# Border between two stages: last core stores from ScalarE's queue, layer 0's gate two turns behind the transposes of x, square roots one turn later

## The chip, the cores and the metric

The kernel runs on one core of a Trainium2 chip. The time is the device time of an execution in microseconds. A core has a matrix engine (TensorE, PE in the profile), a vector engine (VectorE, DVE), an activation engine (ScalarE, ACT), a general engine (GpSimd, POOL) and a queue engine that only issues transfers (SyncE, SP). Each of them takes its own instructions in the order in which the program lists them, and they wait for one another through semaphores. TensorE writes to PSUM[...]; the other data lie in SBUF, and the large arrays in the memory outside.

## The reference

The input x is an array of 384 x 384 positions with 128 channels. Two layers follow each other.

```python
# layer 0
z = layernorm(x)
left  = (z @ Wl + bl) * sigmoid(z @ Wlg + blg)
right = (z @ Wr + br) * sigmoid(z @ Wrg + brg)
core  = einsum('bikh,bjkh->bijh', left, right)
x1 = x + sigmoid(x @ Wg + bg) * (layernorm(core) @ Wout + bout)
# layer 1
left = x1 @ W_left + b_left + x1 @ W_eq + b_eq
out  = left * sum_j(x1 @ W_right + b_right) * sigmoid(x1 @ W_gate + b_gate)
y = layernorm(out @ W_out + b_out + x1)
```

All data are 32-bit floats. The gate `sigmoid(x @ Wg + bg)` of layer 0 needs nothing but x.

## The kernel before

The work is done in three stages, and the order of every engine's instructions is the order of the program (every instruction goes through `seq`, which keeps it).

Stage 1 normalizes x, multiplies it by the four weights of layer 0 (L249), applies the gates (L251, L253) and writes left and right, channel by channel, to `lr_d`. The last two of its result tiles are kept in SBUF (`kept`).

Stage 2 runs over the 128 channels h. `load_h` (L86, L87) brings the channel's left and right from `lr_d`, two channels ahead; `fill` (L316) copies the kept part on GpSimd. Nine pairs of matmuls (L325) make the 384 x 384 core of the channel in PSUM, in one of two buffers of three banks. ScalarE copies it to `ct` (L331) and squares it into `sq` (L333); VectorE adds both to the running sums `csum` and `csq` (L334, L335). Last, SyncE stores `ct` to `core_d` (L337). `ct` has three buffers.

Stage 3 runs over turns t, and each turn works on several rows at once, each at another step. `row(d)` is the row d turns behind. The steps of a row i that matter here are

- turn i: TensorE transposes the row of x (three transposes into `pxt`, L418) and ScalarE copies them to `xT` (L420);
- turn i + 1: TensorE multiplies `xT` by `wg0` into `pg` (L410) and ScalarE makes the gate `gT` (L412);
- turn i + 16: GpSimd multiplies the row's core by the reciprocal deviation into `cs` (L426);
- turn i + 18: TensorE multiplies `cs` by the output weights into `pr` (L453), and VectorE applies the gate and adds x (L454, L456).

The later steps (L469 to L507, up to turn i + 26) are layer 1. Within a turn the gate of the row before stands ahead of the transposes of the row itself. `pg`, `pxt`, `pq`, `pr`, `pg2` and `pl` take turns in four PSUM banks (`bank`). `gT` and `xT` have 20 buffers each. For the first 16 turns TensorE has nothing to do but gates and transposes.

Rows of x come four at a time (`load_x`, L365, four buffers): four loads are issued before turn 0, and one more at each fourth turn. Before turn 5, `rstd` is listed: VectorE makes the variances from `csum` and `csq` (L387 to L389), ScalarE takes their square roots (L390), VectorE makes the reciprocals (L393 to L396), and GpSimd's queue stores them to `rstd_d` (L397). Right behind it come the first two loads of core rows (`load_core`: L370 for `core_d`, L372 for `rstd_d`), both on SyncE. ScalarE's square root and its sigmoid need different function tables, so a table is loaded on either side of the roots.

Of the kernel before, what the change touches and what calls it, by code (L numbers as in the profile page):

```python
# [14 lines left out]
P = 128  # L15
# [4 lines left out]
def triangle_then_gated_row_kernel(ctx: ExitStack, tc: tile.TileContext, a: dict, out: bass.AP):  # L20
# [9 lines left out]
    nc = tc.nc  # L30
# [3 lines left out]
    H = a["L0_conv_Wl"].shape[1]  # L34
# [12 lines left out]
    core_d = dpool.tile([N, H, N], F32, name="core_d")  # L47
    rstd_d = dpool.tile([N, N], F32, name="rstd_d")

    def seq(ins):  # L50

        return tc.keep_in_program_order(ins)
# [21 lines left out]
    with ExitStack() as ctx2:  # L74
# [4 lines left out]
        def load_h(h):  # L79

            if h < H:
                t = inp.tile([P, NB, N, 2], F32, tag="lrh", name="lrh")
                src = lr_d[h].rearrange("(b p) i s -> p b (i s)", p=P)
                i1 = 2 * G * (NG - KEEP)
                dst = t.rearrange("p b i s -> p b (i s)")
                seq(nc.sync.dma_start(out=dst[:, :NB - 1], in_=src[:, :NB - 1]))  # L86
                seq(nc.sync.dma_start(out=dst[:, NB - 1, :i1], in_=src[:, NB - 1, :i1]))  # L87
                loaded2[h] = t
# [215 lines left out]
        with tc.tile_pool(name="p2out", bufs=3, side="right", reuse_waits="tile") as op, \  # L304
             tc.tile_pool(name="p2sq", bufs=2, side="right", reuse_waits="tile") as qp, \
             tc.tile_pool(name="p2ps", bufs=2, space=PSUM, reuse_waits="tile") as ps:
            csum = spool.tile([P, NB, N], F32, name="csum")
            csq = spool.tile([P, NB, N], F32, name="csq")
            seq(nc.vector.memset(csum, 0.0))
            seq(nc.vector.memset(csq, 0.0))  # L310

            def fill(h):

                if h < H:
                    for (kb, ig), lrt in kept.items():
                        seq(nc.gpsimd.tensor_copy(loaded2[h][:, kb, ig * G:(ig + 1) * G, :], lrt[:, h]))  # L316

            fill(0)
            for h in range(H):
                fill(h + 1)  # L320
                t = loaded2.pop(h)
                pc = ps.tile([P, NB, 512], F32, tag="pc", name="pc")
                for kb in range(NB):
                    for ib in range(NB):
                        seq(nc.tensor.matmul(  # L325
                            pc[:, ib, :N], lhsT=t[:, kb, ib * P:(ib + 1) * P, 0], rhs=t[:, kb, :, 1],
                            start=(kb == 0), stop=(kb == NB - 1),
                        ))

                ct = op.tile([P, NB, N], F32, tag="ct", name="ct")  # L330
                seq(nc.scalar.copy(ct, pc[:, :, :N]))  # L331
                sq = qp.tile([P, NB, N], F32, tag="sq", name="sq")
                seq(nc.scalar.activation(sq, ct, AF.Square))  # L333
                seq(nc.vector.tensor_add(csum, csum, ct))  # L334
                seq(nc.vector.tensor_add(csq, csq, sq))  # L335
                load_h(h + 3)
                seq(nc.sync.dma_start(out=core_d[:, h, :].rearrange("(b p) j -> p b j", p=P), in_=ct))  # L337

# [2 lines left out]
    with ExitStack() as ctx3:  # L343
# [18 lines left out]
        def load_x(i0):  # L362
            if i0 < N:
                xt = xin[i0] = xip.tile([P, RG, NB, C], F32, tag="xt", name="xt")
                seq(nc.sync.dma_start(out=xt, in_=x[i0:i0 + RG].rearrange("i (b p) c -> p i b c", p=P)))  # L365

        def load_core(i0):
            if i0 < N:
                ct = inp.tile([P, RG, N], F32, tag="ct", name="ct")
                seq(nc.sync.dma_start(out=ct, in_=core_d[i0:i0 + RG].rearrange("i h j -> h i j")))  # L370
                rt = inp.tile([P, RG, N], F32, tag="rt", name="rt")
                seq(nc.sync.dma_start(  # L372
                    out=rt.rearrange("p i j -> p (i j)"),
                    in_=rstd_d[i0:i0 + RG].rearrange("i j -> (i j)").partition_broadcast(P),
                ))
                cin[i0] = ct, rt

        def rstd():


            def temp(tag, bufs):
                return rp.tile([P, N], F32, tag=tag, name=tag, bufs=bufs)

            w = [(temp("ve", NB), temp("r", NB)) for _ in range(NB)]
            for b, (ve, r) in enumerate(w):
                m = temp("m", 2)
                seq(nc.vector.scalar_tensor_tensor(m, csum[:, b], 1.0 / (H * H), csum[:, b], ALU.mult, ALU.mult))  # L387
                seq(nc.vector.scalar_tensor_tensor(ve, csq[:, b], 1.0 / H, m, ALU.mult, ALU.subtract))
                seq(nc.vector.tensor_scalar(ve, ve, 0.0, EPS, ALU.max, ALU.add))  # L389
                seq(nc.scalar.activation(r, ve, AF.Sqrt))  # L390
            for b, (ve, r) in enumerate(w):
                m = temp("m", 2)
                seq(nc.vector.reciprocal(m, r))  # L393
                seq(nc.vector.tensor_mul(r, m, m))
                seq(nc.vector.scalar_tensor_tensor(r, r, -0.5, ve, ALU.mult, ALU.mult))
                seq(nc.vector.scalar_tensor_tensor(r, r, 1.5, m, ALU.add, ALU.mult))  # L396
                seq(nc.gpsimd.dma_start(out=rstd_d[b * P:(b + 1) * P, :], in_=r))  # L397
# [3 lines left out]
        def tick(t):  # L401

            def row(d):
                return rows.get(t - d)

            r = row(1)
            if r:

                pg = bank("pg")
# [3 lines left out]
            r = row(0)  # L413
# [7 lines left out]
            r = row(A)  # L421
            if r:
                i = t - A
                ct, rt = cin[i // RG * RG]
                cs = r["cs"] = work("cs")
                seq(nc.gpsimd.tensor_tensor(cs, ct[:, i % RG], rt[:, i % RG], ALU.mult))  # L426
            r = row(D)
# [18 lines left out]
            r = row(A + 2)  # L446
# [12 lines left out]
            r = row(A + 6)  # L459
# [5 lines left out]
            r = row(A + 3)  # L465
# [9 lines left out]
            r = row(A + 7)  # L475
# [25 lines left out]
            r = row(A + 9)  # L501
# [9 lines left out]
        for i0 in range(0, 4 * RG, RG):  # L511
            load_x(i0)
        for t in range(N + D):
            if t == 5:
                rstd()
                load_core(0)
                load_core(RG)
            if t < N:
                if t % RG == 0 and t:
                    load_x(t + 3 * RG)  # L520
                rows[t] = {"x": xin[t // RG * RG][:, t % RG]}
            i = t - A
            if i >= 0 and i % RG == 0:
                load_core(i + 2 * RG)
            tick(t)
            i = t - D
            rows.pop(i, None)
            if i >= N - RG:
                seq(nc.sync.dma_start(
                    out=y[i].rearrange("(b p) c -> p b c", p=P), in_=yts[N - RG][:, i % RG]  # L530
                ))
            elif i >= 0 and i % RG == RG - 1:
                i0 = i - RG + 1
                seq(nc.sync.dma_start(out=y[i0:i0 + RG].rearrange("i (b p) c -> p i b c", p=P), in_=yts.pop(i0)))
# [29 lines left out]
```

## Time and profile before

| what | value |
|---|---|
| time, median of 3 runs | 3528.74 us (3528.44 to 3531.65) |
| span of the profiled execution | 3525.9 us |
| TensorE busy | 3460.8 us, 98% |
| VectorE, ScalarE, GpSimd busy | 67%, 55%, 57% |
| mean granted TensorE clock | 0.988 |
| last matmul of stage 2 ends | 1932.04 us |
| first transposes of stage 3 | 1939.96 us |
| first gate matmul (L410) | 1941.73 us |
| first matmul on a core row (L453) | 1994.42 us |

The profile is one execution with the time of each instruction from the start of the span. A group of instructions is named by its line, its engine and its tiles (`pg<-xT` writes pg and reads xT). "PEclk" is the TensorE clock that was granted, as a share of full speed. The chain that ended last is followed back from the last instruction, at each step to whatever released it. SPq is SyncE's queue: the time of an entry is that of issuing a transfer, not that of moving its data.

### The profile page before, as it was taken

To read this page: it belongs to the slowest core of one execution; us is meant where nothing else is said; L and a number is where in the kernel's file an instruction comes from. 1 tells how busy PE (TensorE), PEld (TensorE's weight loads), DVE (VectorE), ACT (ScalarE), POOL (GpSimd) and SP (SyncE) were. 2 spreads that over 40 slices of the span, in tenths; PEclk is the share of its full clock that TensorE was granted. 3 is DMA by queue.
4 is the path that set the end of the run, shared out by engine and by line. 5 is a ranking of instruction groups with operands and counts; after the bars stand their busy time and mean duration, and the time that the engine had idled before them with its cause. 6 is when DMAs were issued, how large, how long until landed. Compare 5 with 4: busy or idle time off the path is not lost.

```text
span 3525.9 us, 48083 instructions
## 1 busy us (share of the span) xinstructions
PE 3460.8 (98%) x13646; PEld 2109.6 (60%) x13646; DVE 2355.9 (67%) x7498; ACT 1946.6 (55%) x3815; POOL 1994.4 (57%) x3529
## 2 busy tenths in 40 slices
PE   7999999999999999999999899999999999999997
PEld 3444444444444555555555477777777777777775
DVE  5666666666666444444444488888888888888887
ACT  3344444444444333333333477777777777777775
POOL 6677777777776000000000277777777777777777
PEclk9999999999999999999999699999999999999999
DMA  3685867768583788888887566666656666666643
GB/s 94 190 228 170 233 183 215 210 186 235 164 234 95 226 272 268 270 269 270 270 269 245 179 204 197 198 201 200 205 192 206 194 201 198 200 202 199 206 162 99
DMA packets 884865, 726.00 MB, mean 206 GB/s; under 512 B 18533, under 2 KB 823017, under 8 KB 884601
## 3 DMA queue, kind: packets, MB, share of 16 engines
q1 hardware_dynamic: 880944, 721.49, 66.3%
q8 instruction: 110, 1.80, 0.2%
q14 instruction: 155, 1.26, 0.1%
q10 hardware_dynamic: 3464, 0.86, 0.1%
q0 software_dynamic: 192, 0.59, 0.0%
HBM read 437.07 MB, written 285.80 MB: 205 GB/s over the span
## 4 chain that ended last, share of the span: by engine, by line
PE 96%; DVE 1%; ACT 1%; DMA 1%; issue 0%; POOL 0%; ACTq 0%; POOLq 0%; SPq 0%
PE pr L249 28%; PE pc L325 22%; PE pg L410 8%; PE pr L453 7%; PE py L485 7%; PE pg L469 7%; PE pl L470 7%; PE pxt L418 4%; PE pt L226 4%; PE py L486 3%; DMA xt<-in_x_dram 1%; ACT py L507 0%; PE pq L443 0%; POOL rs L496 0%; ACT xT L420 0%
## 5 line engine op out<-in xcount | busy, mean ns | idle before, releaser
L249 PE MATMUL pr<-wz,zt 128*128 128x512 f32 x2304 | 1040.8, 594 | 1.1 <-ACT zt L228 1.1
L325 PE MATMUL pc<-lrh 128*128 128x384 f32 x2304 | 779.8, 499 | 1.4 <-DVE lr L253 1.4
L251 ACT ACTIVATE sg<-pr 128x512 f32<-128x512 f32 x576 | 343.9, 597 | 644.6 <-PE pr L249 331.1
L249 PEld LDWEIGHTS pr<-wz,zt 128*128 128x128 f32 x2304 | 416.6, 191 | 415.5 <-issue 414.1
L253 DVE TENSOR_TENSOR lr<-pr,sg 128x512 f32<-128x512 f32 x576 | 398.4, 692 | 378.3 <-ACT sg L251 378.3
L325 PEld LDWEIGHTS pc<-lrh 128*128 128x128 f32 x2304 | 446.9, 194 | 334.5 <-DVE lr L253 2.2
L507 ACT ACTIVATE py<-py,nm,rs 128x128 f32<-128x128 f32 x1152 | 494.1, 429 | 129.5 <-POOL rs L500 94.2
L217 POOL TENSOR_SCALAR z<-xt,rs,sh 128x128 f32<-128x128 f32 x1152 | 497.6, 448 | 0.6 <-POOL z L217 0.4
L334 DVE TENSOR_TENSOR csum<-csum,ct 128x1152 f32<-128x1152 f32 x128 | 173.8, 1358 | 445.0 <-ACT ct L331 445.0
L316 POOL COPY lrh<-lr 128x128 f32<-128x128 f32 x256 | 67.7, 293 | 709.1 <-issue 672.5
L485 PEld LDWEIGHTS py<-wo,u 128*128 128x128 f32 x2304 | 379.0, 191 | 105.7 <-ACT py L507 2.9
L331 ACT COPY ct<-pc 128x1152 f32<-128x1152 f32 x128 | 143.2, 1119 | 486.4 <-PE pc L325 486.4
L485 PE MATMUL py<-wo,u 128*128 128x128 f32 x2304 | 404.9, 275 | 4.3 <-ACT py L507 2.6
L426 POOL TENSOR_TENSOR cs<-ct,rt 128x384 f32<-128x384 f32 x384 | 383.2, 998 | 30.4 <-PE pr L453 30.3
L437 POOL TENSOR_TENSOR yt<-yt,lnb 128x384 f32<-128x384 f32 x384 | 382.6, 996 | 5.0 <-DVE yt L434 4.7
L491 DVE BATCH_NORM_STATS2 st<-py 128x6 f32<-128x128 f32 x1152 | 266.5, 287 | 110.4 <-PE py L486 110.4
L410 PE MATMUL pg<-xT,mat_L_conv_Wg 128*128 128x384 f32 x768 | 326.7, 508 | 12.6 <-ACT xT L420 12.6
L454 DVE SCALAR_TENSOR_TENSOR pr<-pr,bz,gT 128x384 f32<-128x384 f32 x384 | 240.3, 626 | 137.1 <-PE pr L453 136.4
L453 PE MATMUL pr<-cs,wc 128*128 128x384 f32 x768 | 319.8, 498 | 0.0
L486 PE MATMUL py<-ident,x1T 128*128 128x128 f32 x1152 | 314.9, 273 | 0.0
L469 PE MATMUL pg<-x1T,mat_L_conv_W_gate 128*128 128x384 f32 x768 | 311.4, 487 | 3.0 <-DVE x1T L456 2.8
L470 PE MATMUL pl<-x1T,mat_L_conv_W_left 128*128 128x384 f32 x768 | 310.5, 486 | 0.0
(85 smaller groups left out, 4719.5 us busy)
## 6 DMA issues: line engine op xcount, KB each, us to landing
lr_d<-lr SPq DMA_DIRECT2D x128, 1024.0 KB, 9.4
lrh<-lr_d SPq DMA_DIRECT2D x128, 768.0 KB, 4.8
xt<-in_x_dram SPq DMA_DIRECT2D x144, 512.0 KB, 6.0
core_d<-ct SPq DMA_DIRECT2D x128, 576.0 KB, 6.2
xt<-in_x_dram SPq DMA_DIRECT2D x96, 768.0 KB, 4.9
ct<-core_d SPq DMA_DIRECT2D x96, 768.0 KB, 4.7
rt<-rstd_d SPq DMA_DIRECT2D x96, 768.0 KB, 6.1
out_dram<-yt SPq DMA_DIRECT2D x95, 768.0 KB, 4.1
```

The lines of the kernel that those rows point to most:

```text
L217: seq(nc.gpsimd.tensor_scalar(z[:, r, :], xt[:, rr, :], rs[:, rr:rr + 1], sh[:, rr:rr + 1], ALU.mult, ALU.add))
L249: seq(nc.tensor.matmul(pr[:, r, :], lhsT=zt[:, 2 * half + r, :], rhs=wz, start=True, stop=True))
L253: seq(nc.vector.tensor_tensor(t[:, :, i0:i0 + 2, :], pr[:, :, :2 * H].rearrange("k i (h s) -> k h i s", s=2), sg.rearrange("k i (h s) -> k ...
L325: seq(nc.tensor.matmul(pc[:, ib, :N], lhsT=t[:, kb, ib * P:(ib + 1) * P, 0], rhs=t[:, kb, :, 1], start=(kb == 0), stop=(kb == NB - 1),))
L410: seq(nc.tensor.matmul(pg[:, :N], lhsT=wg0, rhs=r["xT"], start=True, stop=True))
L426: seq(nc.gpsimd.tensor_tensor(cs, ct[:, i % RG], rt[:, i % RG], ALU.mult))
L453: seq(nc.tensor.matmul(pr[:, :N], lhsT=wc, rhs=r["cs"], start=True, stop=True))
L469: seq(nc.tensor.matmul(pg2[:, :N], lhsT=wgate, rhs=r["x1T"], start=True, stop=True))
L470: seq(nc.tensor.matmul(pl[:, :N], lhsT=wleft, rhs=r["x1T"], start=True, stop=True))
L485: seq(nc.tensor.matmul(py[:, s], lhsT=r["u"][:, s], rhs=r["wo"], start=True, stop=False))
L486: seq(nc.tensor.matmul(py[:, s], lhsT=r["x1T"][:, s], rhs=ident, start=False, stop=True, is_transpose=True))
L507: seq(nc.scalar.activation(py[:, s], py[:, s], AF.Identity, bias=nm[:, n, b:b + 1], scale=rs[:, n, b:b + 1]))
```

## The change

Three edits, all at the border between stage 2 and stage 3. The core stores of the last three channels (h = 125, 126, 127) are issued by ScalarE instead of SyncE, so that SyncE's queue can go on to the loads of x while stage 2 still runs. The gate of layer 0 is made two turns behind the transposes of its row instead of one, so that TensorE does not have to wait for the copy that was begun just before. And the square roots, with the loads listed after them, come before turn 6 instead of turn 5.

```diff
                 load_h(h + 3)
-                seq(nc.sync.dma_start(out=core_d[:, h, :].rearrange("(b p) j -> p b j", p=P), in_=ct))
+
+                queue = nc.sync if h < H - 3 else nc.scalar
+                seq(queue.dma_start(out=core_d[:, h, :].rearrange("(b p) j -> p b j", p=P), in_=ct))
...
-            r = row(1)
+            r = row(2)
             if r:
 
                 pg = bank("pg")
...
         for t in range(N + D):
-            if t == 5:
+            if t == 6:
                 rstd()
                 load_core(0)
                 load_core(RG)
```

## The prediction

> **What bounds the kernel now.** I read the engine table first: TensorE is busy for nearly the whole span, and the chain that ended last lies on it.
>
> ```profile
> PE 3460.8 (98%) x13646; PEld 2109.6 (60%) x13646; DVE 2355.9 (67%) x7498; ACT 1946.6 (55%) x3815; POOL 1994.4 (57%) x3529
> PE 96%; DVE 1%; ACT 1%; DMA 1%; issue 0%; POOL 0%; ACTq 0%; POOLq 0%; SPq 0%
> PEclk9999999999999999999999699999999999999999
> ```
>
> The reader should see the dip in the clock row: in one fortieth of the span (88 us, around 1940 to 2028) the granted clock falls to six tenths. That is the border between stage 2 (L325) and stage 3, where the change is. So next I read the chain in order of time there (start, length, what).
>
> ```profile
> 1924.93 7.12 PE pc L325 x21
> 1932.08 1.13 ACT ct L331
> 1933.68 6.14 DMA xt<-in_x_dram
> 1939.96 0.89 PE pxt L418 x3
> 1941.20 0.49 ACT xT L420
> 1941.73 1.65 PE pg L410 x2
> 1943.38 0.65 PE pxt L418 x3
> 1944.06 0.49 ACT xT L420
> 1944.59 1.65 PE pg L410 x2
> ...
> 1994.63 1.28 PE pr L453 x2
> 1995.91 0.82 PE pg L410 x2
> 1997.06 0.65 PE pr L453 x2
> ```
>
> Two things are to be seen. First, from the last stage-2 matmul (its end is at 1932.04) to the first gate matmul (1941.73) TensorE does nothing but three transposes: the chain runs through ScalarE's copy of the last core, then through a load of x issued only at 1933.68. Second, from 1941.73 to the first L453 (its record starts at 1994.42, pr of row 0) each turn takes 2.855 us (1941.73, 1944.59, ...): transposes, then ScalarE's copy xT, then the gate that reads this very copy, then the next turn's transposes queued behind that gate. TensorE is held for 0.57 us in every turn. A pair of gate matmuls costs 1.28 us start to start there and 0.65 us after 1996: the array is at half clock all through this stretch.
>
> The timeline of the issuing queue says why the load is late: it stands behind the last core's store, which waits for ct.
>
> ```profile
> 1933.22 0.36 SPq L337 DMA_DIRECT2D core_d<-ct  x1
> 1933.68 16.45 SPq L365 DMA_DIRECT2D xt<-in_x_dram  x5
> ```
>
> Last, the windows of TensorE. Its clock changes at 111.98, 118.81, 1934.70, 1996.14 and 3508.26 us, all on one grid of 3.413 us, so I cut the windows on that grid (columns: stretch, length, TensorE busy, granted clock, DMA share, GB/s).
>
> ```profile
> 115.39:118.81 3.42, 3.42 (x5) 0.50 1.05 296
> 1149.63:1153.05 3.42, 2.01 (x6) 1.00 0.00 0
> 1931.29:1934.70 3.41, 0.75 (x3) 1.00 0.17 63
> 1944.94:1948.35 3.41, 2.84 (x7) 0.50 0.73 184
> 1992.73:1996.14 3.41, 3.41 (x8) 0.50 0.41 166
> ```
>
> After a window 22% busy (1931.29) the clock halves; one 59% busy (1149.63) keeps it full; windows 83% busy by the record (really 1.93 of 2.855 us, 67%) leave it halved; windows busy throughout (115.39, 1992.73) bring it back.
>
> [...]
>
> **The change, part by part.**
>
> *Last three core stores from ScalarE.* They cost nothing for h = 125 and 126: ScalarE is idle 3.77 us per h before L331. For h = 127 the issue comes after the square (1933.23 + 1.16 = 1934.39) and ahead of the first xT. No store from ScalarE is in this stage, so its cost is open: 0 if it is hidden beside the square, 0.36 us as on SyncE, 0.80 us as the longest on GpSimd's L397. I take 0.3. In return SyncE, after the store of h = 124 (issued 1914.95, 0.36 us), goes straight to the x loads. Their tiles lie where the two kept lr tiles lay; the last reader of those is the fill copy of h = 127, at 1913.89 for 0.53 us, and in the trace the first x load has no wait on TensorE. Two of the four may still wait for the last lrh load (issued 1913.84, 4.6 us to landing). All four, 3.1 MB, should land by about 1927, before 1932.04. The lrh load of h = 127 is ahead of them in the same queue. Then TensorE can do two turns of transposes at once, and the first xT starts at 1934.7 (before: 1941.20), the first gate 0.53 us later, at 1935.2 (before: 1941.73).
>
> *Gate two turns behind.* It removes the 0.57 us of waiting: the copy that the gate reads was made a turn earlier. A turn then costs TensorE's own time: at half clock 1.28 + 0.65 = 1.93 us, at full clock 0.65 + 0.33 = 0.98 us. ScalarE's two instructions start 0.48 us apart and fit in either. Four PSUM banks, two used a turn, let TensorE run two turns ahead of ScalarE. From the first gate (turn 2) to pr of row 0 (turn 18) there are 17 such turns. The steady turns are not touched: same order on each engine, and gT is read 16 turns later at L454. The gate dropped from the start comes back as one pair at the end, 0.65 us.
>
> *Square roots one turn later.* The chain in ScalarE is as before, 3.96 us (1953.12 to 1957.08). From the end of turn 5's transposes to the gate of turn 8 is about 0.2 + 0.5 + 4.0 + 0.6 + 0.5 = 5.8 us; two turns hide 3.9 (half clock) or 2.0 (full), so TensorE waits 1.9 or 3.8 us once. VectorE's variances are done at 1940.3 in both kernels. Behind the roots wait rt, ct of the next rows and x(20) in SyncE's queue; x(20) would be issued near 1952.6 and land by about 1963, before turn 20.
>
> *The sum.* If dense turns bring the clock back: half clock from 1935.2 for 1.5 windows on average, 5.1 us, is 2.65 turns; the other 3.35 turns to the end of turn 7 take 3.3 us, to 1943.6. The wait for the roots, 3.8 us, ends at 1947.4 and drops the clock once more: 5.1 us for 2.65 turns, to 1952.5; the last 8.35 turns take 8.2 us. The first pr is at 1960.7, 33.7 us sooner than 1994.42. Before, the clock stayed halved to 1996.14, which returns 0.9 us more; the late gate takes 0.65. Sum: 34 us less, 3528.7 - 34 = 3495.
>
> **The rivals.**
> 1. *The clock stays halved* until pr adds work[...]. Then pr comes at 1935.2 + 17 x 1.93 + 1.9 = 1969.9, 24.5 us sooner, less 0.65: 3505.
> 2. *The clock never drops.* The gap at the border is then only some 2.3 us (1932.9 to 1935.2) and may be split by the grid. The turns would be ready at 1935.2 + 17 x 0.98 + 3.8 = 1955.7. The roots would start near 1941.1; from the first root to the first cs was 14.2 us (1954.41 to 1968.63), so cs is at 1955.3 and pr at 1956.4. That chain becomes the bound: 38 us less, 3490.5.
> 3. *The x loads don't come early*: they wait for stage 2's storage until 1932.1 and take 6.1 us as before. The first xT comes at about 1939.6, 4.9 us later than I think: 3500, or 3510 at half clock.
> 4. *Slower.* If the shifted gate upset the steady turns by 0.1 us each, 384 turns would cost 38 us and eat everything: 3533. For it: those turns fill TensorE to 97% and leave no slack. Against it: no engine's order changes there.
>
> **How the numbers follow.** My sum 0.60, rival 1 0.18, rival 2 0.10, rival 3 0.06, rival 4 0.04, and 0.02 for a gain that is lost within 0.2%. The time is 3495. The range, 3490 to 3506, holds the sum and rivals 1 and 2 with their open parts (store issue 0 to 0.8 us, phase of the clock's grid up to 3.4 us). All cases but the last two end over 0.2% (7 us) faster: 0.94, 0.02, 0.04.
>
> **What would show it.** Right: the x loads issued near 1915 to 1920; the first xT before 1935.5; no wait of L410 on L420 but at the roots; dense turns of 1.9 us, then about 1.0; the first L453 near 1961; the same turn of 3.97 us later. Wrong: x loads issued after 1932, a clock that stays halved to the first pr, L453 waiting for cs, or steady turns longer than before.

## The result and the profile after

The changed kernel takes 3493.08 us (median of 5 runs, 3490.81 to 3496.45) against 3528.74 us; the ratio is 0.9899, with a 95% interval of 0.9884 to 0.9913. The engine table and the clock row of the page after:

```profile
PE 3438.0 (99%) x13646; PEld 2100.7 (60%) x13646; DVE 2356.0 (68%) x7498; ACT 1944.8 (56%) x3815; POOL 1994.5 (57%) x3529
PEclk9999999999999999999999999999999999999999
```

The dip of the clock row is gone, and TensorE is busy for 22.8 us less with the same number of matmuls: matmuls of the border now run at full clock (a pair of gate matmuls takes 0.65 us from start to start, before 1.28). The chain in order of time at the border (line numbers are two higher than before from L339 on: the gate is L412, pr L455; entries of `issue` and of ACTq are not shown, and dots stand for longer stretches):

```profile
1933.07 1.13 ACT ct L331
1934.22 0.37 ACT sq L333
1935.30 0.47 ACT xT L422
1935.81 0.91 PE pg L412 x2
1936.72 0.33 PE pxt L420 x3
1937.05 0.65 PE pg L412 x2
...
1940.65 1.28 ACT L392
1941.95 1.35 ACT r L392 x3
1943.31 1.28 ACT L414
...
1945.61 0.91 PE pg L412 x2
```

And from the timeline, the last core store on ScalarE's queue and the first pr (in brackets its engine's idle time before it and what ended that):

```profile
1934.23 0.37 ACTq L339 DMA_DIRECT2D core_d<-ct  x1
1957.23 0.91 PE L455 MATMUL pr<-cs,wc 128*128 128x384 f32 x2 [0.62 <-POOL cs L428]
```

In this execution stage 2 ended at 1933.04, 1.0 us later than in the trace before. From there to the first gate it is 2.77 us (before 9.69), and after a first turn of 1.08 us the turns follow each other at 0.97 to 0.98 us. ScalarE's block of two table loads of 1.28 us each and three roots in 1.35 us between them (1940.65 to 1944.59) is what TensorE waits for in the middle, once, for 3.68 us. The first pr starts at 1957.23, 24.2 us after the end of stage 2; before it was 62.4. From the first pr to the end of the span it is 1531.8 us, before 1531.4: all of the gain lies in the border.

SyncE's queue shows the early loads, directly behind the store of h = 124:

```profile
1915.95 0.36 SPq L339 DMA_DIRECT2D core_d<-ct  x1
1916.41 22.01 SPq L367 DMA_DIRECT2D xt<-in_x_dram  x5
```

The second entry joins five issues. The four early ones end at 1926.55; the fifth, for a later turn, begins at 1938.05.

And TensorE's windows on the clock's grid, which in this execution has boundaries at 1933.63 and 1937.04, since the clock changes at 110.91, 121.15, 3469.63, 3476.46 and 3479.87, all whole steps of 3.413 us apart (stretch, length, TensorE busy, granted clock, DMA share, GB/s):

```profile
1933.63:1937.04 3.41, 1.78 (x9) 1.00 0.82 294
1937.04:1940.46 3.42, 3.42 (x18) 1.00 0.25 62
1940.46:1943.87 3.41, 1.47 (x9) 1.00 1.12 347
1943.87:1947.28 3.41, 1.67 (x7) 1.00 0.15 51
```

The gap at the border leaves its window 52% busy, and the grid cuts the wait for the roots into two windows of 43% and 49%. The granted clock is 1.00 through all of them.

### The profile page after: what moved, and what is told of

Same layout as the page of the kernel before. It is cut to its first block, busy times and chain, and to the rows that moved or that the text cites. A ratio compares the mean times of both kernels' runs of the same rounds, so it can differ in the third digit from the quotient of the medians.

```text
span 3489.0 us, 48077 instructions
## 1 busy us (share of the span) xinstructions
PE 3438.0 (99%) x13646; PEld 2100.7 (60%) x13646; DVE 2356.0 (68%) x7498; ACT 1944.8 (56%) x3815; POOL 1994.5 (57%) x3529
## 4 chain that ended last, share of the span: by engine, by line
PE 96%; DVE 1%; ACT 1%; DMA 1%; POOL 0%; issue 0%; SPq 0%; ACTq 0%; POOLq 0%; DVEq 0%
PE pr L249 28%; PE pc L325 22%; PE pr L455 7%; PE pg L412 7%; PE py L487 7%; PE pl L472 7%; PE pg L471 7%; PE pt L226 4%; PE pxt L420 3%; PE py L488 3%; DMA xt<-in_x_dram 1%; ACT py L509 0%; PE pq L445 0%; POOL rs L498 0%; DVE yt L436 0%
## 5 line engine op out<-in xcount | busy, mean ns | idle before, releaser
L455 PE MATMUL pr<-cs,wc 128*128 128x384 f32 x768 | 319.2, 497 | 0.6 <-POOL cs L428 0.6
L412 PE MATMUL pg<-xT,mat_L_conv_Wg 128*128 128x384 f32 x768 | 311.6, 487 | 4.7 <-ACT xT L422 4.7
```

Of the source, the lines that this page charges most:

```text
L412: seq(nc.tensor.matmul(pg[:, :N], lhsT=wg0, rhs=r["xT"], start=True, stop=True))
L455: seq(nc.tensor.matmul(pr[:, :N], lhsT=wc, rhs=r["cs"], start=True, stop=True))
```

## The experiments

The end of stage 2 lay between 1929.5 and 1936.2 us in the twelve traces, though nothing differs ahead of it but the queue of three stores. So the traces are compared from that end on. Times are medians of several runs; the other columns come from one trace of each kernel, and the end is the start of the last instruction, 0.05 us ahead of the end of the span.

| kernel | time | to the first gate | to the first pr | first pr to the end | clock halved at border or roots |
|---|---|---|---|---|---|
| before | 3528.74 | 9.69 | 62.39 | 1531.39 | from the border to the first pr |
| changed | 3493.08 | 2.77 | 24.19 | 1531.76 | no |
| stores alone | 3520.52 | 2.77 | 55.46 | 1531.49 | from the border to the first pr |
| gate alone | 3501.08 | 9.67 | 34.69 | 1530.71 | twice, border and roots |
| gate and roots | 3499.48 | 9.69 | 34.57 | 1530.70 | twice |
| roots alone | 3530.25 | 9.67 | 62.37 | 1531.48 | from the border to the first pr |
| before, with filler matmuls | 3514.42 | 9.67 | 48.81 | 1530.89 | twice |
| changed, roots before turn 5 | 3489.50 | 2.77 | 25.10 | 1530.79 | once, roots |
| changed, loads reordered | 3490.96 | 2.77 | 25.10 | 1530.83 | once, roots |
| changed, second trace | 3492.92 | 2.77 | 24.94 | 1532.35 | once, roots |
| changed, third trace | 3493.51 | 2.77 | 25.09 | 1531.38 | once, roots |
| four turns behind | 3490.84 | 2.77 | 23.00 | 1531.20 | once, roots |

My theory was that two things are saved, waiting and time at half clock. The rivals were that the early loads are the whole gain, that only the waits count, and that dense turns leave the clock halved.

**The stores alone.**

```diff
-                seq(nc.sync.dma_start(out=core_d[:, h, :] ...
+                queue = nc.sync if h < H - 3 else nc.scalar
+                seq(queue.dma_start(out=core_d[:, h, :] ...
```

> Only the last three core stores go to ScalarE; gate one turn behind and roots before turn 5 as before. My theory (two separate things are saved: waiting, and time at half clock) expects the first gate some 6 us sooner, the turns with their waits as before. If the clock still drops in the gap between the last core and the first gate (now about 2.9 us), the turns stay at 2.855 us and the time is about 3522 us (6 less). If it doesn't drop, the turns are about 1.75 us and the time about 3503. The rival, that the early loads alone are the gain, expects 3493.

Ratio 0.9976 (0.9967 to 0.9985), 8 us less. Its chain in order of time (line numbers are one higher than before):

```profile
1933.79 0.47 ACT xT L421
1934.30 1.65 PE pg L411 x2
1935.95 0.66 PE pxt L419 x3
1936.63 0.49 ACT xT L421
1937.16 1.65 PE pg L411 x2
```

The reader sees the start 6.9 us sooner and, in the two gates at 1934.30 and 1937.16, the old turn of 2.86 us. One window at the border was 34% busy; the clock fell at its end and stayed halved for 54.6 us. All eleven runs lie between 3518.5 and 3525.2 us, none near the 3503 us expected for a clock that keeps full. So the early loads alone are about a fifth of the gain. The gap has the same length as in the changed kernel, 2.77 us, but the second turn's transposes stand behind the gate and don't fill it (34% of the window busy, 52% there); that this is why the clock drops here and not there is read from the traces, not tested by itself.

**The gate alone, and gate with roots.**

```diff
-            r = row(1)
+            r = row(2)
...
-            if t == 5:
+            if t == 6:
```

> Only the gate is two turns behind; stores on SyncE, roots before turn 5. TensorE is idle for 8 us at the border as before, so the clock drops for certain. If dense turns bring it back within one or two windows of 3.413 us: first pr about 1967, time about 3502 us. If [...]dense turns leave it halved: turns of 1.93 us to the first pr, which comes near 1976, time about 3511. The rival, that only the early start keeps the clock, expects 3511 too, with the clock at half in the whole fill; the turns tell.

> Gate two turns behind and roots before turn 6, the stores still on SyncE (the change without its first part). The roots' place matters little: within 2 us of the kernel with the gate alone, so 3502 if dense turns restore the clock, 3511 if they don't. Against the changed kernel (3493) this prices the stores: 6 us of start plus whatever the clock's drop costs.

Ratios 0.9918 (0.9904 to 0.9933) and 0.9916 (0.9901 to 0.9931). The windows of the kernel with gate and roots:

```profile
1941.28:1944.69 3.41, 3.16 (x7) 0.50 1.17 291
1948.10:1951.52 3.42, 1.10 (x7) 1.00 1.09 332
1954.93:1958.35 3.42, 3.42 (x10) 0.50 0.32 90
```

The clock, lost in the wait for x, is back after the window from 1941.28, which was 93% busy and held nothing but gates and transposes. The wait for the roots leaves 32% of the window from 1948.10 busy and drops the clock again; it is back after the window from 1954.93, 100% busy. That refutes the rival in which dense turns of gates and transposes leave the clock halved, and the times of both kernels are near the 3502 us expected for this case. What the two drops cost can be read from the steps from gate to gate: 2.08 and 1.52 us at the start instead of 1.08 and 0.97, and 2.08, 1.92 and 1.71 behind the roots instead of 1.08, 0.97 and 0.98. That is 1.5 us for the first drop and 2.7 us for the second.

**The kernel before with filler matmuls.** In turns 0 to 17 a matmul whose result nothing reads stands behind the transposes; no part of the change is made.

```diff
                 seq(nc.scalar.copy(xT, pxt[:, :N]))
+                if 0 <= t < 18:
+                    pf = ps2.tile([P, 512], F32, tag="py", name="pf")
+                    seq(nc.tensor.matmul(pf[:, :256], lhsT=wg0, rhs=wz[:, :256], start=True, stop=True))
```

> The kernel before, plus one matmul pair of 256 columns per turn behind the transposes in turns 0 to 17, into a py bank that nothing reads: it computes nothing that is used, it only fills the 0.57 us in which TensorE waits. No part of the change is made. If the clock is a cause of its own: after one or two dense windows it is full, the turns fall from 2.855 to about 1.75 us although they hold more work, and the time is about 3511 (17 less). The rival, that only the waits count, expects no gain: 3529 or up to 5 us more.

Ratio 0.9958 (0.9943 to 0.9973): with more work, 14 us less. From its chain:

```profile
1957.91 0.93 PE pg L410 x2
1958.86 0.58 ACT gT L412
1959.44 0.38 ACT xT L420
1959.86 0.93 PE pg L410 x2
```

Most turns fell from 2.86 to 1.95 us: the clock is a cause of its own. My 1.75 us was too low: with the gate one turn behind, ScalarE makes gT before xT, so gate, sigmoid, copy and next gate form one chain, 0.93 + 0.58 + 0.38 us and small gaps. From the first gate to the first pr it is 52.7 us before, 39.1 with the filler and 21.4 with the change: of the 31.3 us, the clock accounts for at least 13.6, since the filler kernel itself is at half clock for three windows from the border on and for one at the roots. The other 17.7 us are the shorter chain, what these two drops cost, and one turn less, because the changed kernel's first gate stands in turn 2 and not in turn 1. These three weren't separated.

**The roots' place.**

> Only the roots move one turn later, all else as before. The turns are bound by the transposes, the copy and the gate, and cs is ready 24 us before it is needed: no difference, 3528 us within 2.

> The change without its last part: stores on ScalarE, gate two turns behind, roots before turn 5. VectorE has the variances of all three blocks by about 7.9 us after the last core's matmul, and turn 5 begins at about 5.9 us, with a table load of 1.28 us ahead of the roots; so the third root may wait a little, and cs comes about 1 us sooner. I expect no difference against the changed kernel (within 2 us, 3491 to 3495). The rival, that the roots' place is needed for the gain, expects a wait of ScalarE for VectorE at the roots and 3 us or more lost.

One turn later alone makes no difference (ratio 1.0003, 0.9994 to 1.0011). The change with the roots left before turn 5 takes 3489.50 us (0.9891, 0.9875 to 0.9908), not slower than with them at turn 6: this part of the change isn't needed for the gain. VectorE was no hindrance. From the end of stage 2 to the end of the span it is 1555.9 us, and 1556.0, 1557.3 and 1556.5 in the three traces of the changed kernel. With the roots at turn 5, TensorE doesn't wait for the load of x for turn 20, as it does in all three of those (see below), and from the first pr to the end it is 1530.8 us. So the later place of the roots may even cost about 1 us; the times can't settle that.

**The changed kernel's second trace.**

> The changed kernel once more, for a second trace. The grid on which the clock is decided lies anew against the border in each execution. My theory: where a grid window holds nearly all of TensorE's wait for the roots (3.7 us) or of the gap at the border (about 2.4 us idle of 2.8), the clock drops there and the first pr comes up to 4 us later than in the first trace (24.2 us after the last core's matmul); else it is the same. Time 3490 to 3497.

```profile
1944.25:1947.66 3.41, 0.00 (x1) 1.00 0.76 249
1947.66:1951.08 3.42, 3.15 (x7) 0.50 0.08 31
```

From the end of stage 2 to the next boundary of the grid it is 2.66 us in the trace before, 0.59 in the first trace of the changed kernel and 2.1 with the gate alone. Here the grid lay so that one window held the whole wait for the roots. The clock fell at its end and was back one window later, after 92% busy; the first pr came 0.75 us later than in the first trace, not the 4 us that were allowed for at most. The third trace (below) shows the same: first pr 0.9 us later.

**The loads reordered.** In the first two traces of the changed kernel TensorE waits for the load of x for turn 20, 0.9 and 1.6 us. In SyncE's queue it stands behind a load of `rstd_d` that waits for GpSimd's store, 10.3 us in the first of them. Here those first two loads come later (the part of `load_core` that becomes `load_rstd` is left out).

```diff
             if t == 6:
                 rstd()
-                load_core(0)
-                load_core(RG)
+                load_core(0, True)
+                load_core(RG, True)
...
                     load_x(t + 3 * RG)
+                if t == 8:
+                    load_rstd(0)
+                if t == 12:
+                    load_rstd(RG)
```

> The changed kernel, with the first two loads of the reciprocal deviations listed behind the loads of x for turns 20 and 24 (in turns 8 and 12) instead of ahead of them, so that SyncE's queue doesn't hold x(20) until GpSimd's store has landed. The last theory of what is still lost behind the fill: TensorE's wait of 0.9 us for that x load goes away, x(20) is issued near 10 us after the last core's matmul instead of 18. The wait for cs (0.6 us) stays. 1 us less than the changed kernel, which the time can hardly show; the waits do.

```profile
1936.52 0.37 SPq L367 DMA_DIRECT2D xt<-in_x_dram  x1
1936.99 2.25 SPq L372 DMA_DIRECT2D ct<-core_d  x2
1940.43 0.37 SPq L367 DMA_DIRECT2D xt<-in_x_dram  x1
1949.23 0.33 SPq L381 DMA_DIRECT2D rt<-rstd_d  x1
```

The load of x(20) is issued at 1940.43, 8.9 us after the end of stage 2 (18.0 in the changed kernel), ahead of rt. The wait for it is gone. The wait for cs, expected to stay, doesn't show either, since the clock dropped at the roots and the first pr came at 25.1 us. From the first pr to the end it is 1530.8 us instead of 1531.8, 1532.4 and 1531.4 in the three traces of the changed kernel. The kernel with the roots before turn 5 reaches 1530.8 as well, without this edit. The time, 3490.96 us, can't tell any of this from the scatter.

**Four turns behind.** With the reordered loads, the roots before turn 5, and pxt in the py banks while these are idle:

```diff
-            r = row(2)
+            r = row(4)
...
-                pxt = bank("pxt")
+                pxt = bank("pxt") if t >= A + 2 else ps2.tile([P, 512], F32, tag="py", name="pxt")
```

> The changed kernel with the gate four turns behind, pxt in the four py banks (idle until turn 23) for the turns before 18, roots before turn 5, and the loads reordered. Theory: TensorE's wait for the roots shrinks from 3.7 to about 1.9 us since it can run four turns ahead, too short to drop the clock in any phase of the grid; the first pr then comes 23 to 24 us after the last core's matmul (24.2 to 25.1 so far), bounded by cs, and the x load is not waited for. 1 to 3 us less than the changed kernel: 3488 to 3491. The rival, that cs already bounds all of it, expects no gain at all over the kernel with the loads reordered.

> The changed kernel on the same chip as the kernel with the deeper lag, for the comparison of the two: 3490 to 3497, the first pr 24.2 to 25 us after the last core's matmul, according to where the grid of the clock lies.

3490.84 us (0.9889, 0.9874 to 0.9904) beside 3493.51 us (0.9898, 0.9881 to 0.9914) for the changed kernel: the intervals overlap. In the trace the first pr is at 23.0 us, as expected, but the step was wrong: the wait for the roots fell only to 3.2 us, not to 1.9, and the clock dropped all the same. ScalarE had come so early that it waited 1.2 us for VectorE's variances. At the end of the fill pr still waited 0.2 us for cs. The rival was that cs already bounds all of it, with no gain over the reordered loads. In the traces it is 1554.2 us from the end of stage 2 to the end of the span, 1.7 less than with the reordered loads; the times, 3490.84 and 3490.96 us, show no difference. So this stays open.

## Why the prediction held, point by point

The forecast was 3495 us, measured were 3493.08. The mechanism was right: the early loads, the shorter chain, and a clock that dense turns bring back (with gate and roots alone after a window 93% busy). The parts did not all come as forecast, and that the number lies within 2 us is in part luck (last paragraph of this section).

- *The x loads come early*: right, from 1916.41. They did not land by about 1927, as the sum has it: the second to fourth took 3.7, 3.3 and 2.6 us each to issue, against 0.43 for the first, and the third landed at 1931.71. TensorE waited for none of the four. The rival that they wait for stage 2's storage fell.
- *The first xT at 1934.7, the first gate at 1935.2*, which is 3.2 us after the end of stage 2: measured 2.77. The term for the store's issue was too large. ScalarE's queue issues it in 0.37 us from 1934.23, beside the square; its cost is 0, not 0.3.
- *Half clock from 1935.2 for 1.5 windows*: this step failed. In all six traces that have both the early loads and a gate two or more turns behind, the clock outlived the border. The wait was short, and the second turn's transposes fell into it, so the window was 52% busy in the first trace and 49 to 65% in the other five. The forecast had the gap right in rival 2, and gave it too small a chance.
- *Turns of 1.93 and 0.98 us*: right, 1.92 and 0.97 to 0.98. The text calls the waiting that goes 0.57 us; that is the idle time by the record. The sum rightly takes off 0.93 (2.855 less 1.93), because a gate pair, recorded with 1.65 us, takes only 1.28 where the next matmuls stand ready.
- *A wait of 3.8 us for the roots, and a drop of the clock there*: the wait is right (3.68 us). The drop depends on the grid: none in the first trace of the changed kernel, one in the other two. Its size was too large: 5.1 us at half clock was assumed, and it was one window of 3.4 us in the second and third trace. The drop falls late in the wait or up to 1.2 us behind it, and the clock was back after the next window, 92% and 100% busy. The second and third trace lose 0.75 and 0.9 us at the first pr.
- *The first pr*: 28.7 us after the end of stage 2 in my sum, 24.4 in rival 2, measured 24.2 to 25.1. Rival 2, that the clock never drops, is what happened in the first trace, and as it said, pr then waits for cs, 0.6 us. In the other two the clock held at the border, as in rival 2, and dropped at the roots, as in the sum.
- *x(20) before turn 20*: wrong. The turns were faster than in the sum, and the load took 11.5 us from its issue until it released TensorE. The wait, 0.6 to 1.6 us in the three traces, takes back part of what the first pr gained.
- *The gate that comes back at the end, 0.65 us*: the traces show next to nothing of it. From the pr of row 340 to that of the last row it is 159.47 us before and 159.51 with gate and roots alone. The time that the clock's return gives behind the first pr was forecast as 0.9 us; over the first 20 rows it is 0.76 (73.82 before, 73.06 with gate and roots).

In the first trace the first pr is 38.2 us sooner, and the part behind it 0.4 us longer: 37.8 us, 3.8 more than forecast; the second and third trace have 36.5 and 37.3 from the end of stage 2 on. Most of what the sum lacked is the border: 2.65 turns at half clock in 5.1 us, which at full clock take 2.6 (an estimate from 0.98 us a turn), a difference of 2.5 us. The medians differ by only 35.7, so they lie nearer to the forecast than the traces do. The scatter of the end of stage 2 (1932.0 before, 1933.0 to 1936.2 in the three traces of the changed kernel) covers that difference; its cause stays open.

## What to carry to other kernels

Here the stretch of many short turns at half clock cost two terms: the wait in each turn (0.57 us), and the doubled length of TensorE's own work (a pair of gate matmuls 1.28 us instead of 0.65), since with these waits in it the clock stayed halved to 1996.14; with the waits filled it was back after a window 99% busy. Shifting a consumer by one more turn removed both here, and moving loads ahead in their queue kept the gap before it short; to the first pr, the two together gave 38.2 us in the first trace and 37.3 to 37.5 in the others, against 6.9 + 27.8 for the two alone. The times don't show that excess: 35.7 us together, 8.0 and 29.1 alone. Before pricing a gap on TensorE, cut the trace on the clock's grid and look at how busy each window is.

## What was not expected of the hardware

The prediction had a drop of the clock after a window 22% busy and full clock kept after one 59% busy; the runs fill the range between. The start of the span, where the trace before has full clock with TensorE 0 to 6% busy up to 16.4 us, is set aside. Cut on the grid of 3.413 us, the twelve traces have drops after windows 0 to 50% busy by the record and full clock kept after windows from 43% busy on; at the border and the roots alone all drops lie at 37% and below, and all windows that kept the clock at 43% and above. So the clock also fell after windows that were a third busy (34% at the border with the stores alone, 37% with the gate alone), and between 43 and 50% it did either. On the way up it came back after windows 81 to 100% busy, and stayed halved after windows 83% busy in the kernel before and once after one of 93%. What tells these cases apart was not shown; the busy share by the record, whose matmul ends are modelled, does not. A third of the work in the turns that restored the clock at the border were transposes (0.65 of 1.93 us); they did not keep it from coming back.
